# A shared expert's up product done with seven half-size products, its down products set between the next group's

## The chip, the cores and the metric

The kernel runs on one core of one Trainium2 chip. The metric is the device time of one execution in microseconds (us), lower is better. A profiled execution also leaves a trace; the times of all instructions in this document are from such executions, and windows are given in us from the start of the span.

The engines are TensorE (PE, with its weight loads shown apart as PEld), VectorE (DVE), ScalarE (ACT), GpSimd (POOL) and SyncE (SP, which here only issues transfers).

## The reference, cut to what matters

All tensors are float32. The input is x of 4 x 512 tokens of 512 values, so T = 2048 tokens and D = 512.

```python
# 1. a feed-forward layer whose expert (one of 4) goes by the token's id
h = layernorm(x)
x = x + where(expert_of(token_id) == e, (silu(h @ Wg[e].T) * (h @ Wu[e].T)) @ Wd[e], ...)   # Wg = Wu = Wd = ctx
# 2. a mixture of 32 experts, four a token, and a shared expert that all tokens pass
h = rmsnorm(layernorm(x), norm_w)
weights, ids = top_k(softmax(h @ gate_w), 4)
routed = sum over the four of weight * (silu(h @ w13[e][:, :256]) * (h @ w13[e][:, 256:])) @ w2[e]
shared = silu(h @ shared_gate_w) * (h @ shared_up_w) @ shared_down_w    # 512 -> 256 -> 512
out = x + routed + shared + layernorm(x)
```

The residual inside the second layer is its own normalised input, so the output is the sum of x, that input, the routed and the shared part. An expert takes at most a fixed number of tokens; the data here stay below it.

## The kernel before, in words

The 2048 tokens are 16 tiles of 128, and four tiles make a group (GT = 4, G = 4 groups of 512 tokens). There are three stages on the time axis.

**Cross attention layer, 0 to 173 us.** `xattn` (L499) loops over 19 blocks b of 128 tokens that share an expert. For each block TensorE makes `up(b)` (L453, `pp`, 32 instructions of 128 columns), then `down(b)` (L476, `po`, 512 columns), with transposes (`turn_block`, `tp`) between. VectorE makes the tokens' moments (`x_moments`, L336 to L339), copies the transposed tokens (`xT<-tp`, L450), the product `aT<-s,pp` (L474) and the sum into `acc` (L494). From block 5 on the second layer's start is woven in: `settle`, `norm` (L595, L607: the norms, whose powers POOL makes at L605), `turn_row` (L619, transposes to `h2T`, one tile per group, kept for all four groups), and for each finished group the routing: `route` (L648, 16 gate matmuls into `pc`, a ScalarE copy to `lT`), `choose` (L663, the transpose `pl` and the top four), `spread`, `count` (`pn`) and `number`, which give each token its slot in the experts' table.

**Shared expert, 173 to 269 us.** For each group, `glu_up` (L832) makes for the two halves f of the 256 inner values the gate product `pg` and the up product `pu`: four matmuls of 512 columns each over the four chunks c of D, so 16 a group, 4 x 128 x 512 multiplications each. ScalarE makes silu of `pg` (L847), VectorE the product with `pu` (L848, tile `aT_s`). Then `shared` (L860) makes the four tiles' down products (`glu_down`, L851, two matmuls of 512 columns a tile), which VectorE adds into `acc` (L864). The last group's transposes, routing and `ranks` (L775, the order of the experts by load, a long chain of small VectorE instructions) are called between group 0's up and down products. TensorE's order, like that of each engine, is made by a scheduler from the calls' order, so transposes, logits and downs of group 0 stand mixed.

Rows go to the experts' table (`s_dram`) by indirect transfers that POOL issues: `scatter_one(j, k)` (L754) sends tile j's rows to their k-th expert's slots, and `base(j)` (L764) sends a finished tile of `acc` to the output. In this stage they wait in a list `to_put`; `step(product)` (L770) takes the next from the list and has it wait for that product. `glu_up` calls it after every second matmul and `glu_down` after every tile, so 12 times a group.

**Ranks, 269 to 634 us.** The loop over 32 experts in order of load (L1214) takes each expert's rows (`fetch`, on SP's queue), transposes them on VectorE (L971), makes the up products (`up_rank`, L1041, 256 columns at most) and the down products (`down_rank_by_halves`, L1071), which already replace eight half products by seven with sums on VectorE. The results go out by POOL. Its weights come on SP's queue into the pools `wts_a` and `wts_b`, several ranks ahead. `wts_b` and `last` open when the pools of the shared stage close.

Two notes on tiles: `shw13` holds the shared gate and up weights side by side (128 x 4 x 512) and `shw2` the down weights; `ps_m` are three banks of PSUM (2 KB a partition), `ps_o` two and `ps_t` two.

Of the kernel before, what the change touches and what calls it, by code (L numbers as in the profile page):

```python
# [8 lines left out]
F32 = mybir.dt.float32  # L9
# [8 lines left out]
P = 128  # L18
# [41 lines left out]
def tile_xattn_moe(  # L60
# [38 lines left out]
    tok_sb = const.tile([P, NT], I32, name="tok_sb")  # L99
    nc.sync.dma_start(tok_sb, tok)  # L100
    acc = keep.tile([P, NT, D], F32, name="acc")
    cT = ctx_pool.tile([P, EX, DC, D], F32, name="cT")

    def context(e):
# [5 lines left out]
    nwq = const.tile([P, DC], F32, name="nwq")  # L110
    shw13 = keep.tile([P, DC, 2 * I], F32, name="shw13")
    shw2 = keep.tile([P, IC, D], F32, name="shw2")

    none = ctx_pool.tile([P, NB, RW], F32, name="none")

    def second_inputs(after_):

# [123 lines left out]
    nc.vector.tensor_reduce(xrow, xv.rearrange("p e t -> p t e"), AX.X, ALU.add)  # L241
    xblk, xq = split(xrow, ctx_pool, "x", F16)

    xa = ctx_pool.tile([P, NT, P], F16, name="xa")
    xbt = ctx_pool.tile([P, NT, NT], F16, name="xbt")
    xb16 = ctx_pool.tile([P, NT, NT], F16, name="xb16")
    nc.vector.tensor_tensor(
# [251 lines left out]
    def xattn():  # L499
        def fetched(*js):  # L500
            for j in js:
                x_block(j)

        fetched(0, 1, 2)
        for b in range(2):
            loaded = x_registers(b)
            with tc.issue_after(loaded) if loaded is not None else nullcontext():
                st = x_moments(b)
            behind(st, scaled if b else planned)
            if not b:  # L510
# [24 lines left out]
        for b in range(XB):  # L535
            j = GT * (b // 2 + 1)
            if j < NT and b % 2 == 0:
                for i in range(j, j + GT):
                    st = x_moments(i)
                    if i == GT:  # L540
                        behind(st, made[0])
                x_root(j, GT)
                if j == GT:
                    fetched(*range(2 * GT, NT))
                    second_inputs(st)
                    blanks(loads[-1])
            if b + 3 < XB:
                x_norm(b + 3)
                if not b:
                    behind(powers[-1], made[0])  # L550
            if 0 < b < XB - 2:
                hold(b + 2)
            if b + 1 < XB:
                up(b + 1, range(DC // 2))

            g, i = divmod(b - (XB - NT) - GT - 2, GT)
            if i == 0 and g >= 0:
                choose(g, ups_[-1])
# [12 lines left out]
            if j >= 1:  # L571
                norm(j - 1)
            if j >= 0:
                settle(j)
            if j >= GT + 4:
                scatter(j - GT - 4)
            for late_, what in ((3, spread), (4, number)):
                if j >= late_ and (j - late_) % GT == GT - 1:
                    if what is number:
                        count((j - late_) // GT)  # L580
                    what((j - late_) // GT)


    hs, h2T, tops = {}, {}, {}
    row_puts, out_puts, out_puts_l = [], [], []
    tails = []
# [61 lines left out]
    def route(g):  # L648

        pc = ps_t.tile([P, P], F32, tag="tp", name="pc")  # L650
        for c in range(DC):
            for i in range(GT):
                nc.tensor.matmul(
                    pc[i * E : (i + 1) * E, :],
                    gate_sb[:, c, :],
                    h2T[g][:, c, i * P : (i + 1) * P],
                    start=(c == 0),
                    stop=(c == DC - 1),
                )
        lT = tops[g] = mid.tile([P, P], F32, tag="lT", name=f"lT{g}")  # L660
        nc.scalar.copy(lT, pc)
# [102 lines left out]
    def base(j):  # L764
        return put_rows(out, xtok[:, j : j + 1], acc[:, j, :], out_puts, "base")
# [63 lines left out]
    HD = D // 2  # L829
    muls_s, adds_s = [], []  # L830

    def glu_up(xT, w13t, name):  # L832
        aT = cols.tile([P, IC, GT * P], F32, tag="aT", name=f"aT_{name}")
        for f in range(IC):
            pg = ps_m.tile([P, GT * P], F32, tag="mm", name="pg")
            pu = ps_m.tile([P, GT * P], F32, tag="mm", name="pu")
            for ps, fo in ((pg, f), (pu, IC + f)):
                for c in range(DC):
                    ins = nc.tensor.matmul(
                        ps, w13t[:, c, fo * P : (fo + 1) * P], xT[:, c, :], start=(c == 0), stop=(c == DC - 1)  # L840
                    )
                    if c % 2:
                        step(ins)
            if f == 0:
                first_half = ins
            s = mid.tile([P, GT * P], F32, tag="silu", name="s")
            nc.scalar.activation(s, pg, AF.Silu)  # L847
            muls_s.append(nc.vector.tensor_tensor(aT[:, f, :], s, pu, ALU.mult))  # L848
        return aT, first_half

    def glu_down(aT, w2t, i):  # L851
        po = ps_o.tile([P, D], F32, tag="po", name="po")
        for f in range(IC):
            ins = nc.tensor.matmul(  # L854
                po, aT[:, f, i * P : (i + 1) * P], w2t[:, f, :], start=(f == 0), stop=(f == IC - 1)
            )
        step(ins)
        return po

    def shared(g, aT):  # L860
        for i in range(GT):
            j = g * GT + i
            po = glu_down(aT, shw2, i)
            adds_s.append(nc.vector.tensor_tensor(acc[:, j, :], acc[:, j, :], po, ALU.add))  # L864
            to_put.append(lambda j=j: base(j))


    def blanks(after_):

        n = NS // (P * NB)  # L870
        ins = nc.sync.dma_start(
            s_dram[:NS, :].rearrange("(n p j) w -> p n (j w)", j=NB, p=P),
            none.rearrange("p j w -> p (j w)").unsqueeze(1).to_broadcast([P, n, NB * RW]),
        )
        behind(ins, after_, mybir.DependencyClass.Sync)

    xattn()
    aT_s = {}
    to_put.extend(lambda j=j, k=k: scatter_one(j, k) for j in range(NT - GT - 4, NT - GT) for k in range(K))
    aT_s[0], up_s = glu_up(h2T[0], shw13, "s0")  # L880
    rank_x = rank_rows(adds_x[-1])
    norm(NT - 1)
    turn_row(NT - 2, downs[-1])
    turn_row(NT - 1, up_s)
    route(G - 1)
    choose(G - 1)
    spread(G - 1)
    count(G - 1)
    number(G - 1)
    to_put.extend(lambda j=j, k=k: scatter_one(j, k) for j in range(NT - GT, NT) for k in range(K))  # L890
    first.close()
    late = ctx.enter_context(tc.tile_pool(name="late", bufs=2))
    wts_a = ctx.enter_context(tc.tile_pool(name="wts_a", bufs=2))
    third = ctx.enter_context(ExitStack())
    slots = third.enter_context(tc.tile_pool(name="slots", bufs=1))
    er, er_x, er_i, over_i = ranks()
    for g in range(G):
        if g:
            aT_s[g], _ = glu_up(h2T[g], shw13, f"s{g}")
        shared(g, aT_s[g])  # L900
    while to_put:
        to_put.pop(0)()

# [347 lines left out]
    with tc.If(need > 0):  # L1251
# [17 lines left out]
            return oh  # L1269

        def gathered(table, index, width, tag, name):
            pool = late if tag == "xg_x" else last
# [131 lines left out]
```

## Time and profile before

| what | us |
|---|---|
| median of three runs | 646.26 |
| lowest, highest | 644.96, 646.71 |
| the profiled execution | 647.86 |
| its span | 646.0 |
| TensorE busy in the span | 608.7 |
| VectorE busy | 397.3 |
| POOL busy | 246.2 |
| ScalarE busy | 216.0 |
| first shared product (L839) starts | 172.74 |
| last shared down product ends, rank 0's first matmul (L1050) starts | 268.76 |

The span runs from the first to the last instruction of the trace; 1.86 us of the execution lie around it. In a line of a timeline the first number is the start in us, the second the time from the first to the last of so many instructions (x8) that follow each other, then engine, line of the kernel, operation, what it writes and reads, and its size; in brackets stands how long the engine sat idle before it and what ended that wait. In a line of a table of windows, the busy time of the five rows PE, PEld, DVE, ACT and POOL follows the window, each with its number of instructions, then TensorE's granted clock as a share of full speed, the DMA engines' mean busy share and the GB/s moved.

### The profile page before, as it was taken

The numbers are of one execution on the slowest core, as the hardware profiler recorded it, in microseconds if no ns is written. First come the engines' busy times: TensorE is split into PE (matmuls) and PEld (weight loads), VectorE is DVE, ScalarE is ACT, GpSimd is POOL, SyncE is SP. The second block draws the span as 40 slices with busy tenths as digits, with TensorE's granted clock in tenths as the row PEclk, the third lists the DMA queues.
The fourth block names the chain that finished last, engine by engine and source line by source line (L and its number), as shares of the span: only waits on it lengthen the run. The fifth ranks groups of instructions, "written<-read, shape, count | busy, mean of one in ns | idle before, by whom it ended". The sixth has DMA issues, their size and how long they took to land. (4 is left out here: it accounts for less than half of the span.)

```text
span 646.0 us, 10595 instructions
## 1 busy us (share of the span) xinstructions
PE 608.7 (94%) x2962; PEld 433.5 (67%) x2962; DVE 397.3 (61%) x1113; ACT 216.0 (33%) x390; POOL 246.2 (38%) x217
## 2 busy tenths in 40 slices
PE   5899999999997999999999999999999999999990
PEld 2777767776543444566767687677678888888870
DVE  7655457575725712756667567667668777778730
ACT  2444765764322000122323222322333333333320
POOL 4451101365673555433234324324324232323331
PEclk9999999999997999999999999999999999999996
DMA  7489991335272697698979979979999999999442
GB/s 260 135 309 413 413 415 70 133 118 216 99 269 104 195 375 210 197 319 165 288 154 260 258 151 241 275 160 244 275 265 278 281 261 274 239 247 229 62 55 37
DMA packets 104453, 144.57 MB, mean 224 GB/s; under 512 B 21184, under 2 KB 58048, under 8 KB 101824
## 3 DMA queue, kind: packets, MB, share of 16 engines
q1 hardware_dynamic: 86400, 101.54, 53.6%
q0 software_dynamic: 17984, 42.26, 27.0%
q8 instruction: 26, 0.43, 0.3%
q14 instruction: 43, 0.35, 0.2%
HBM read 79.05 MB, written 66.22 MB: 225 GB/s over the span
## 5 line engine op out<-in xcount | busy, mean ns | idle before, releaser
L1022 POOL DMA_INDIRECT out<-eo,to_all x64 | 100.5, 1570 | 228.9 <-DVE eo L1091 111.3
L1050 PE MATMUL pg<-xT,w 128*128 128x256 f32 (+2 forms) x512 | 135.2, 377 | 0.0
L1050 PE MATMUL pu<-xT,w 128*128 128x256 f32 (+2 forms) x512 | 114.9, 376 | 0.0
L1088 ACT ACTIVATE eo<-po,wt 128x256 f32<-128x256 f32 x124 | 58.6, 474 | 158.5 <-PE po L1085 120.0
L1050 PEld LDWEIGHTS pg<-xT,w 128*128 128x128 f32 x512 | 96.5, 190 | 17.7 <-issue 5.4
L1050 PEld LDWEIGHTS pu<-xT,w 128*128 128x128 f32 x512 | 97.2, 190 | 12.2 <-issue 0.8
L636 POOL DMA_INDIRECT s_dram<-h,slot x64 | 62.2, 973 | 35.4 <-issue 15.4
L458 PEld LDWEIGHTS pp<-xT,held 128*128 128x128 f32 x576 | 66.8, 192 | 8.3 <-issue 5.2
L458 PE MATMUL pp<-xT,held 128*128 128x128 f32 x576 | 68.2, 276 | 1.4 <-DVE xT L450 0.8
L479 PE MATMUL po<-cT,aT 128*128 (+1 forms) x152 | 68.6, 593 | 0.3 <-issue 0.3
L971 DVE STREAM_TRANSPOSE xT<-z 128x1024 f32<-128x1024 f32 x32 | 65.3, 2041 | 3.8 <-DMA z<-s_dram 3.8
L1091 DVE SCALAR_TENSOR_TENSOR eo<-po,wt,eo 128x256 f32<-128x256 f32 x93 | 44.7, 482 | 16.2 <-PE po L1085 9.8
L1057 DVE TENSOR_TENSOR aT_r<-s,pu 128x256 f32<-128x256 f32 (+2 forms) x64 | 26.4, 414 | 41.0 <-PE pu L1050 35.4
L981 ACT ACTIVATE xT<-xT,nwq 128x256 f32<-128x256 f32 x64 | 29.1, 502 | 59.7 <-DVE xT L971 43.1
L479 PEld LDWEIGHTS po<-cT,aT 128*128 128x128 f32 x152 | 27.3, 190 | 27.9 <-issue 27.9
L1068 DVE TENSOR_TENSOR t_r<-w,t_r 128x256 f32<-128x256 f32 x62 | 26.3, 424 | 31.6 <-PE po L1085 29.0
L1085 PE MATMUL po<-t_r,aT_r 128*128 128x256 f32 x124 | 38.1, 389 | 2.0 <-DVE eo L1091 1.5
L605 POOL TENSOR_TENSOR rs<-rs,mhalf 128x2 f32<-128x2 f32 x16 | 11.3, 706 | 74.8 <-DVE rs L604 74.8
L1085 PE MATMUL po<-w,aT_r 128*128 128x256 f32 x124 | 39.7, 401 | 0.0
L389 ACT COPY held<-cT 128x1024 f32 x36 | 36.0, 1048 | 10.3 <-DVE valid L306 10.0
L1085 PE MATMUL po<-t_r,s_r 128*128 128x256 f32 x124 | 37.8, 387 | 0.4 <-DVE eo L1091 0.2
L854 PE MATMUL po<-shw,aT_s 128*128 128x512 f32 x64 | 32.3, 644 | 1.4 <-issue 1.0
(203 smaller groups left out, 765.2 us busy)
## 6 DMA issues: line engine op xcount, KB each, us to landing
w<-in_w SPq DMA_DIRECT2D x192, 256.0 KB
s_dram<-none SPq DMA_DIRECT2D x1, 20840.0 KB
z<-s_dram SPq DMA_DIRECT2D x128, 128.0 KB
h_dram<-h SPq DMA_DIRECT2D x4, 1042.0 KB
cT<-in_ctxT SPq DMA_DIRECT2D x4, 1024.0 KB
out<-none SPq DMA_DIRECT2D x1, 1024.0 KB
s_dram<-h,slot POOLq DMA_INDIRECT x64
out<-eo,to_all POOLq DMA_INDIRECT x64
```

The source lines that it names most:

```text
L389: ins = nc.scalar.copy(held[b][:, h : h + n], cT[:, bass.ds(e, 1), h : h + n].rearrange("p o c f -> p (o c) f"))
L458: ins = nc.tensor.matmul(ups[b][:, f, :], held[b][:, c, f * P : (f + 1) * P], xT_[b][:, c, :], start=(f == 0 and c == 0) if b == 0 else (c ...
L479: ins = nc.tensor.matmul(po, aT_[b][:, f, :], cT[:, bass.ds(off[b], 1), f, :].rearrange("p o f -> p (o f)"), start=(f == 0), stop=(f == DC ...
L636: put = nc.gpsimd.indirect_dma_start(out=table, out_offset=bass.IndirectOffsetOnAxis(ap=index, axis=0), in_=src, in_offset=None,)
L854: ins = nc.tensor.matmul(po, aT[:, f, i * P : (i + 1) * P], w2t[:, f, :], start=(f == 0), stop=(f == IC - 1))
L971: ins = nc.vector.transpose(xT.rearrange("p c (r b) -> p r c b", b=SQ), z.rearrange("p r (a c) -> p r c a", c=DC))
L981: nc.scalar.mul(xT[:, c, :], xT[:, c, :], nwq[:, c : c + 1])
L1022: put = nc.gpsimd.indirect_dma_start(out=out, out_offset=bass.IndirectOffsetOnAxis(ap=dst, axis=0), in_=eo, in_offset=None, bounds_check=T ...
L1050: last_up = nc.tensor.matmul(ps, w13t[:, c, f * P : (f + 1) * P], xT[:, c, :n], start=(c == 0), stop=(c == DC - 1))
L1085: return nc.tensor.matmul(ps, L[i], R[i], start=first_, stop=True, skip_group_check=True)
L1088: nc.scalar.mul(eo[i][:, j, :], ps, wt[:, i : i + 1])
L1091: nc.vector.scalar_tensor_tensor(eo[i][:, j, :], ps, wt[:, i : i + 1], eo[i][:, j, :], ALU.mult, ALU.add)
```

## The change

The up product of a group is seen as one matrix product: the weights, 512 values by 512 columns (256 gate, 256 up), against 512 values by 512 tokens. Both are cut in two by two blocks: the weights by halves of D and by gate and up, the tokens by halves of D and by halves of the group. Seven products of blocks (each 256 values x 256 columns x 256 tokens) with sums before and after them replace the eight that the plain product has. A product is four matmuls of 256 columns, so a group has 28 of them in place of 16 of 512 columns.

What moves with it:

- `shared_weights` makes four sums of weight blocks on VectorE, once, called at block 6 of the cross attention (one of them in place over a block of `shw13`).
- `shared_tokens(g)` makes for each group four sums of token blocks on VectorE, one of them at product 2 and two in place over blocks of `h2T`.
- `glu_up(g)` is now a generator of six steps. It uses three banks: ScalarE copies banks to `c11`, `c22`, `c12`, VectorE adds the next bank to the copy, and bank `u1` is accumulated over products 1, 6, 7 and 4.
- `shared(g, i)` makes one tile's down product, in the order 2, 3, 0, 1; each stands after one step of the next group's generator.
- `step` is called after each half product (14 a group) and after each down product (4), so 18 times a group.
- The pools `late`, `wts_a` and `slots` open, and the first stage's pool closes, ahead of the shared stage; a new pool `sums` holds the sums and copies. `none` and `xa` are only allocated earlier, and one buffer for a part that does not run here moves to `slots`.

```diff
@@ xattn, loop over b @@
+            if b == 6:
+                weight_sums.update(shared_weights())
@@
-    def glu_up(xT, w13t, name):
...
-    def glu_down(aT, w2t, i):
...
+    def shared_weights():
+        (a11, a12), (a21, a22) = [
+            [shw13[:, 2 * k : 2 * k + 2, i * I : (i + 1) * I] for k in range(2)] for i in range(2)
+        ]
+        s1, s2, s4 = [cols.tile([P, 2, I], F32, name=f"su{i}", bufs=1) for i in (1, 2, 4)]
+        plus(s1, a21, a22)
+        less(s2, s1, a11)
+        less(s4, a12, s2)
+        less(a21, a11, a21)
+        return {1: a11, 2: a12, 3: s4, 4: a22, 5: s1, 6: s2, 7: a21}
+
+    def shared_tokens(g):
+        (b11, b12), (b21, b22) = [
+            [h2T[g][:, 2 * k : 2 * k + 2, j * HALF : (j + 1) * HALF] for j in range(2)] for k in range(2)
+        ]
+        t1, t2 = [sums.tile([P, 2, HALF], F32, tag=f"st{i}", name=f"st{i}_{g}") for i in (1, 2)]
+        less(t1, b12, b11)
+        less(t2, b22, t1)
+        less(b12, b22, b12)
+        return {1: b11, 2: b21, 3: b22, 4: b21, 5: t1, 6: t2, 7: b12}
+
+    def product(ps, i, R, first_=False):
+        w = weight_sums[i]
+        for f in range(2):
+            for c in range(2):
+                ins = nc.tensor.matmul(
+                    ps[:, f, :],
+                    w[:, c, f * P : (f + 1) * P],
+                    R[i][:, c, :],
+                    start=first_ and f == 0 and c == 0,
+                    stop=f == 1 and c == 1,
+                    skip_group_check=True,
+                )
+            step(ins)
+        return ins
+
+    def glu_up(g):
+        R = tokens_s[g]
+        b1 = bank("u1")
+        product(b1, 1, R, True)
+        c11 = held_sum(b1, "c11")
+        yield
+        b2 = bank("u2")
+        product(b2, 2, R, True)
+        less(R[4], R[4], R[6])
+        plus(c11, c11, b2)
+        nc.scalar.activation(c11, c11, AF.Silu)
+        yield
+        b3 = bank("u3")
+        ins = product(b3, 5, R, True)
+        c22 = held_sum(b3, "c22")
+        yield ins
+        product(b1, 6, R)
+        c12 = held_sum(b1, "c12")
+        yield
+        product(b3, 3, R)
+        plus(c12, c12, b3)
+        nc.scalar.activation(c12, c12, AF.Silu)
+        product(b1, 7, R)
+        plus(c22, c22, b1)
+        aT = aT_s[g] = cols.tile([P, IC, GT * P], F32, tag="aT", name=f"aT_s{g}", bufs=1)
+        muls_s.append(nc.vector.tensor_tensor(aT[:, :, HALF:], c12, c22, ALU.mult))
+        yield
+        product(b1, 4, R)
+        if g + 1 < G:
+            tokens_s[g + 1] = shared_tokens(g + 1)
+        muls_s.append(nc.vector.tensor_tensor(aT[:, :, :HALF], c11, b1, ALU.mult))
+        yield
@@ after xattn() @@
+    first.close()
+    late = ctx.enter_context(tc.tile_pool(name="late", bufs=2))
+    wts_a = ctx.enter_context(tc.tile_pool(name="wts_a", bufs=2))
+    third = ctx.enter_context(ExitStack())
+    sums = third.enter_context(tc.tile_pool(name="sums", bufs=1))
+    slots = third.enter_context(tc.tile_pool(name="slots", bufs=1))
     to_put.extend(lambda j=j, k=k: scatter_one(j, k) for j in range(NT - GT - 4, NT - GT) for k in range(K))
-    aT_s[0], up_s = glu_up(h2T[0], shw13, "s0")
+    tokens_s[0] = shared_tokens(0)
+    ups_s = [glu_up(g) for g in range(G)]
+    next(ups_s[0])
+    next(ups_s[0])
+    up_s = next(ups_s[0])
+    next(ups_s[0])
     rank_x = rank_rows(adds_x[-1])
     norm(NT - 1)
     turn_row(NT - 2, downs[-1])
     turn_row(NT - 1, up_s)
+    next(ups_s[0])
     route(G - 1)
...
     er, er_x, er_i, over_i = ranks()
+    next(ups_s[0])
     for g in range(G):
-        if g:
-            aT_s[g], _ = glu_up(h2T[g], shw13, f"s{g}")
-        shared(g, aT_s[g])
+        for i in (2, 3, 0, 1):
+            if g + 1 < G:
+                next(ups_s[g + 1])
+            shared(g, i)
+        if g + 1 < G:
+            next(ups_s[g + 1])
+            next(ups_s[g + 1])
```

More of the change, by code (lines that the diff above doesn't have):

```diff
@@ L101, in tile_xattn_moe @@
     acc = keep.tile([P, NT, D], F32, name="acc")
+    none = ctx_pool.tile([P, NB, RW], F32, name="none")
+    xa = ctx_pool.tile([P, NT, P], F16, name="xa")
     cT = ctx_pool.tile([P, EX, DC, D], F32, name="cT")
@@ L112, in tile_xattn_moe @@
     shw2 = keep.tile([P, IC, D], F32, name="shw2")
-    none = ctx_pool.tile([P, NB, RW], F32, name="none")
     def second_inputs(after_):
@@ L242, in tile_xattn_moe @@
     xblk, xq = split(xrow, ctx_pool, "x", F16)
-    xa = ctx_pool.tile([P, NT, P], F16, name="xa")
     xbt = ctx_pool.tile([P, NT, NT], F16, name="xbt")
@@ L581, in xattn @@
                     what((j - late_) // GT)
+    weight_sums = {}
     hs, h2T, tops = {}, {}, {}
@@ L830, in tile_xattn_moe @@
     muls_s, adds_s = [], []
-    def glu_up(xT, w13t, name):
[L833 to L849, printed above, removed]
@@ L851, in glu_down, with plus, less @@
-    def glu_down(aT, w2t, i):
+    HALF = GT * P // 2
+    HD = D // 2
+    def plus(dst, x_, y_):
+        return nc.vector.tensor_tensor(dst, x_, y_, ALU.add)
+    def less(dst, x_, y_):
+        return nc.vector.tensor_tensor(dst, x_, y_, ALU.subtract)
+    def shared_weights():
[8 more added lines that the diff above has]
+        return {1: a11, 2: a12, 3: s4, 4: a22, 5: s1, 6: s2, 7: a21}
@@ new lines, in bank, with held_sum @@
+    def bank(name):
+        return ps_m.tile([P, 2, HALF], F32, tag="mm", name=name)
+    def held_sum(ps, name):
+        t = sums.tile([P, 2, HALF], F32, tag=name, name=name)
+        nc.scalar.copy(t, ps)
+        return t
+    def glu_up(g):
[30 more added lines that the diff above has]
+        yield
@@ L852, in glu_down, with shared @@
+    def shared(g, i):
+        j = g * GT + i
         po = ps_o.tile([P, D], F32, tag="po", name="po")
@@ L854, in glu_down @@
             ins = nc.tensor.matmul(
-                po, aT[:, f, i * P : (i + 1) * P], w2t[:, f, :], start=(f == 0), stop=(f == IC - 1)
+                po, aT_s[g][:, f, i * P : (i + 1) * P], shw2[:, f, :], start=(f == 0), stop=(f == IC - 1)
             )
         step(ins)
[L858 to L865, printed above, removed]
+        adds_s.append(nc.vector.tensor_tensor(acc[:, j, :], acc[:, j, :], po, ALU.add))
+        to_put.append(lambda: base(j))
     def blanks(after_):
@@ L877, in tile_xattn_moe @@
     xattn()
-    aT_s = {}
-    to_put.extend(lambda j=j, k=k: scatter_one(j, k) for j in range(NT - GT - 4, NT - GT) for k in range(K))
-    aT_s[0], up_s = glu_up(h2T[0], shw13, "s0")
+    first.close()
[4 more added lines that the diff above has]
+    slots = third.enter_context(tc.tile_pool(name="slots", bufs=1))
+    aT_s, tokens_s = {}, {}
+    to_put.extend(lambda j=j, k=k: scatter_one(j, k) for j in range(NT - GT - 4, NT - GT) for k in range(K))
+    tokens_s[0] = shared_tokens(0)
[4 more added lines that the diff above has]
+    next(ups_s[0])
     rank_x = rank_rows(adds_x[-1])
@@ L890, in tile_xattn_moe @@
     to_put.extend(lambda j=j, k=k: scatter_one(j, k) for j in range(NT - GT, NT) for k in range(K))
[L891 to L895, printed above, removed]
     er, er_x, er_i, over_i = ranks()
+    next(ups_s[0])
     for g in range(G):
-        if g:
-            aT_s[g], _ = glu_up(h2T[g], shw13, f"s{g}")
-        shared(g, aT_s[g])
+        for i in (2, 3, 0, 1):
[5 more added lines that the diff above has]
+            next(ups_s[g + 1])
     while to_put:
@@ L1271, in gathered @@
         def gathered(table, index, width, tag, name):
-            pool = late if tag == "xg_x" else last
+            pool = slots if tag == "xg_x" else last
             rows = pool.tile([P, 1, width], F32, tag=tag, name=name, bufs=2 if tag == "xg_x" else EO)
```

## The prediction, as written before the result was known

> **What bounds the kernel now.** I read the page's busy shares first, then a table of windows, then TensorE's timeline through the stage that the change touches, then the three engines around one hole in it.
>
> ```profile
> PE 608.7 (94%) x2962; PEld 433.5 (67%) x2962; DVE 397.3 (61%) x1113; ACT 216.0 (33%) x390; POOL 246.2 (38%) x217
> PEclk9999999999997999999999999999999999999996
> ```
>
> TensorE is busy for 94% of the span, and its granted clock has one dip, in the thirteenth slice of 16 us. The windows (PE, PEld, DVE, ACT, POOL, clock, DMA share, GB/s) place both:
>
> ```profile
> 180.00:200.00 20.00, 14.13 (x66) 6.53 (x66) 3.95 (x11) 4.48 (x9) 12.03 (x13) 0.92 0.60 227
> 200.00:220.00 20.00, 20.00 (x46) 8.76 (x45) 17.39 (x59) 2.69 (x4) 8.08 (x9) 0.91 0.32 123
> 220.00:240.00 20.00, 20.00 (x48) 8.72 (x47) 3.93 (x6) 1.20 (x2) 13.09 (x14) 1.00 1.02 363
> 240.00:260.00 20.00, 20.00 (x47) 8.66 (x46) 4.12 (x6) 1.20 (x2) 10.77 (x12) 1.00 0.71 216
> 300.00:320.00 20.00, 20.00 (x91) 13.47 (x90) 12.68 (x30) 5.23 (x11) 7.31 (x5) 1.00 1.02 233
> ```
>
> The shared stage (173 to 269) has TensorE full from 200 on; VectorE is full only from 200 to 220, with the routing and the ranks. The rank phase behind it has TensorE full too, although its DMA share stands near 1. TensorE's timeline gives the prices:
>
> ```profile
> 226.50 3.60 PE L839 MATMUL pg<-h2T,shw 128*128 128x512 f32 x8
> 229.93 3.60 PE L839 MATMUL pu<-h2T,shw 128*128 128x512 f32 x8
> 268.76 3.62 PE L1050 MATMUL pg<-xT,w 128*128 128x256 f32 x16
> 272.21 2.97 PE L1050 MATMUL pu<-xT,w 128*128 128x256 f32 x13
> ```
>
> A float32 matmul is two instructions here. Eight of 512 columns take 229.93 - 226.50 = 3.43 us, 0.858 per matmul; sixteen of 256 take 272.21 - 268.76 = 3.45, 0.431 per matmul. Half the columns cost half the time.
>
> ```profile
> 192.13 1.38 PE L854 MATMUL po<-shw,aT_s 128*128 128x512 f32 x2 [1.01 <-issue]
> 198.27 0.47 PE L667 MATMUL pl<-ident,lT 128*128 128x128 f32 x1 [4.75 <-ACT lT L661]
> 197.95 0.27 ACT L661 COPY lT<-pc 128x128 f32<-128x128 f32 x1 [8.35 <-remote]
> 196.00:198.00 2.00, 0.00 (x0) 0.00 (x0) 0.00 (x0) 0.05 (x1) 0.00 (x0) 0.71 0.34 133
> ```
>
> This is the hole. The copy of the last group's logits waits for a signal until 197.95, though the logits' matmuls are shown ending at 191.1; TensorE stands for 4.75 us, and no engine computes between 196 and 197.9. The other three groups' copies (93.7, 127.6, 161.3) came 1.2 us or less after their matmuls. I do not know the cause.
>
> **The change, part by part.** The sum is made on the profiled execution, 647.86 us (span 646.0 and 1.86 around it), which is 1.60 above the median of the runs, 646.26.
>
> 1. *Products.* A group had 16 matmuls of 512 columns, 16 x 0.858 = 13.73 us; it gets 7 x 4 of 256, 28 x 0.431 = 12.07. That is -1.66 for each of 4 groups, -6.6 in all, in a stage where TensorE is the bound. The 32 down matmuls stay.
>
> 2. *The hole.* From 191.12 (pc's end) to 193.51, TensorE did one matmul worth 0.86, so 1.5 lost; then 4.75; then the granted clock is 0.5 from 196.82 to 203.65, of which TensorE works 198.27 to 203.65, 5.4 us at half rate, 2.7 lost. Together 9.0. In the changed order the last group's logits follow product 7 and its two transposes, one matmul and then the transpose pl stand behind them, and the scatters beside them are in other places. Bounds: 0 (it comes again) and -9.0. I take -9.0 for the likeliest case, since three of four such copies ran without it, and give the other end a case of its own.
>
> 3. *Waits that go.* The down products waited 1.9 us in total for the last aT (weight loads of L854, 3 times) and TensorE itself 1.4; another group's products now stand between. -1.5.
>
> 4. *Waits that come*, by the changed order of each engine. (a) Tile 15's transposes wait for h, whose mean and root on VectorE and POOL now stand behind token sums of 0.69 us: 1.2 (0 to 2.5). (b) pl, own and the two pn meet less cover, since half products of 1.7 us stand where 3.4 us blocks stood: 2.0 (0.7 to 3). (c) Group 1's product 4 needs its bank read by the sum of c22, which on VectorE is queued behind what is left of the ranks chain: 1.7 (0.5 to 3.0, beyond that see the rivals). (d) The last group has no next group between its products 7 and 4 and its downs: 1.0 (0.3 to 1.5), from a sum of 0.69 and its hand-over. (e) Bank hand-overs: bank u1 is written by products 1, 6, 7 and 4 in turn, each after a reader of 0.6 to 0.69 us; in every group some five new hand-overs, mostly behind a down or another product. Nothing in the trace before has this form; the nearest row is the 0.28 us that a down product waited for an acc sum at 266.94. 20 x 0.1 = 2.0 (0 to 6). Sum +7.9 (1.5 to 16).
>
> 5. *Weight sums.* Four VectorE operations of 0.69 us, put by the scheduler into blocks 2 and 3 of the cross attention:
>
> ```profile
> 36.91 0.68 DVE L474 TENSOR_TENSOR aT<-s,pp 128x512 f32<-128x512 f32 x1
> 39.17 0.69 DVE L494 TENSOR_TENSOR acc<-acc,po 128x512 f32 x1 [1.59 <-PE po L479]
> 44.02 0.68 DVE L450 COPY xT<-tp 128x512 f32<-128x512 f32 x1
> 46.09 3.73 PE L458 MATMUL pp<-xT,held 128*128 128x128 f32 x32
> ```
>
> Three come after the mult at 36.91, where VectorE idles 1.59; three take 2.0, so the sum at 39.17 slips by some 0.5 and the copy xT, with the fourth, by up to 1.2. It ends at 44.7 and is needed at 46.09, so 1.4 of slack covers it. But they also wait for the gate's and the up weight's loads, whose transfers the queue's bytes put at about 36.4, an estimate; if these are late, x_moments, the xT copy and TensorE are late by as much. +0.8 (0 to 2.5).
>
> 6. *At nothing.* Token sums, bank sums and copies: VectorE 6 x 0.69 = 4.1 us a group more, ScalarE 3 copies and the same silu work, 1.8 more, beside 19 us of TensorE a group; VectorE has over 15 of 20 free from 220 on. Between 200 and 220 it has 2.6, which is why (c) is there. Scatters: 18 steps a group for 12, each 0.96 us on POOL's queue at 1.27 apart, so POOL alone now paces them; the last of s_dram moves from 240.7 to about 227, and the first fetch of z, at 243.5 on SP's queue, with it. The first transpose of z is at 262, so earlier gains nothing, and a delay of some 10 us would still be covered. Behind the scatters on POOL stand only tile 15's roots (in (a)) and the base rows. Pools that open earlier: SP's rank weights come some 9 us sooner; hidden.
>
> 7. *The way to the end.* The rank phase takes a shift whole if TensorE bounds it: it is busy 19.4 to 20 of 20 there, and waits 2.1 us in total for weights. So -6.6 - 9.0 - 1.5 + 7.9 + 0.8 = -8.4: 639.5 in a profiled execution, 637.9 against the median.
>
> [...] The row is 4.75 us of standing and then 6.83 us at 0.5. [...]
>
> **Rivals.** *The hole comes again* (0.30): its place, logits then one matmul then pl, keeps its form. While all stand, VectorE works off its queue, so (c) and part of (b), 2.0, are hidden: -8.4 + 9.0 - 2.0 = -1.4, 644.9, with +-2.
>
> *VectorE holds TensorE in the routing* (0.15, slower). In the trace, the routing and ranks run without a gap from 208.29 to 219.8, 11.5 us. If (c) waits for the whole chain, TensorE stands 11.5 in place of 1.7, and after a stand like the 4.75 above the clock halves, 5.4 us at half rate, 2.7: +12.5, 650.4. It decides from 5.7 + 1.7 = 7.4 us of standing on. For it: 17.39 of 20 busy. Against: between the ranks' pn and product 4 stand four products and three downs, 7 x 1.72 = 12 us of cover.
>
> *DMA sets the rank phase* (0.08): its share is 0.97 to 1.02 in several windows. Ranks that start earlier then wait for weights; half the gain stays, 642.0. Against: weights are issued four to five ranks ahead, paced by TensorE itself.
>
> **How the numbers follow.** The likeliest, 0.47, is 637.9; its own range, from the bounds of 4 and 5 without all falling one way, 634 to 642. Cases: 0.47, all faster by over 0.3% (1.94 us, about what a measurement here can tell from none); 0.30 around 644.9, of which 0.13 faster, 0.12 same, 0.05 slower; 0.08 at 642, 0.07 faster; 0.15 slower. Faster 0.67, same 0.13, slower 0.20. Below 634 lie 0.06, above 648.5 some 0.13, so the range is 634 to 648.5.
>
> **What would show it.** Right: L871 with 224 instructions of about 0.215 us; rank 0's first matmul near 260 instead of 268.76; no TensorE wait over 3 us and no half clock in 185 to 215; the same 365 us from there to the end. Wrong: a wait of ScalarE's copy lT for over 3 us (the hole); product 4 of group 1 waiting for VectorE over 3 us; L458 in block 3 starting after 46.9; weights waited for more than 2.1 us in the ranks.

## The result, and the profile after

The changed kernel takes 663.32 us (median of four runs, 660.92 to 665.68) against 646.49 (644.96 to 647.17) for the kernel before: a ratio of 1.0264, with a 95% interval of 1.0221 to 1.0306. It is slower by 16.8 us, where 8.4 us of gain were forecast. The kernel before itself takes about 637 us in some comparisons, called prompt below, and 644 to 648 in others, called late, and this first comparison is a late one, so every number stands beside that of the kernel before from the same comparison.

The changed kernel's profiled execution took 660.92 us, its span 659.1. Its page opens with

```profile
PE 607.7 (92%) x3058; PEld 455.0 (69%) x3058; DVE 415.1 (63%) x1145; ACT 223.0 (34%) x402; POOL 251.3 (38%) x217
PEclk9999999999987979999999999999999999999997
```

TensorE has about as much busy time as before (607.7 for 608.7), although its products need 6.6 us less, since more of its work runs at half clock. The table of windows (PE, PEld, DVE, ACT, POOL, clock, DMA share, GB/s) shows where:

```profile
180.00:200.00 20.00, 11.76 (x76) 9.04 (x75) 8.87 (x39) 6.37 (x12) 15.53 (x16) 0.80 0.65 250
200.00:220.00 20.00, 15.23 (x46) 10.14 (x46) 13.43 (x36) 3.65 (x6) 5.32 (x6) 0.86 0.22 85
220.00:240.00 20.00, 15.07 (x59) 10.84 (x58) 8.36 (x22) 1.45 (x3) 14.80 (x15) 1.00 0.97 333
240.00:260.00 20.00, 16.12 (x51) 10.62 (x52) 8.48 (x13) 2.81 (x5) 9.09 (x9) 0.83 0.70 236
```

Before, TensorE was busy for 20.00 of 20 from 200 to 260. Now it lacks four to eight in each window, and the clock falls in three, to a granted 0.50 (in the windows 193 to 201, 209.3 to 212.6 and 240 to 246): (1 - 0.80) x 20 x 2 = 8.0 us at half rate, then 5.6, then 6.8, 20.4 in all for 6.8 before. TensorE's timeline has the stands:

```profile
186.78 0.70 PE L871 MATMUL u<-h2T,shw 128*128 128x256 f32 x2
195.06 0.48 PE L669 MATMUL pl<-ident,lT 128*128 128x128 f32 x1 [7.58 <-issue]
195.33 1.92 PE L871 MATMUL u<-h2T,shw 128*128 128x256 f32 x4
197.93 4.60 PE L871 MATMUL u<-h2T,shw 128*128 128x256 f32 x10
209.45 0.19 PE L719 MATMUL pn<-own,tri 128*128 128x32 f16 x1 [4.77 <-DVE own L711]
233.18 1.89 PE L871 MATMUL u<-st,su 128*128 128x256 f32 x8
242.24 3.78 PE L928 MATMUL po<-shw,aT_s 128*128 128x512 f32 x4 [7.17 <-issue]
249.81 1.98 PE L928 MATMUL po<-shw,aT_s 128*128 128x512 f32 x4 [1.64 <-DVE acc L932]
284.62 3.62 PE L1130 MATMUL pg<-xT,w 128*128 128x256 f32 x16
```

The stage from the first shared product to rank 0's first matmul takes 284.62 - 173.27 = 111.4 us, for 96.0 before. The ranks behind it take 361.4 for 360.4 and the tail behind TensorE's last matmul 13.0 for 16.9. The stage also starts 0.5 us later. Together 0.5 + 15.3 + 1.0 - 3.9 = 12.9, which is the 13.1 us between the two spans but for rounding: the loss lies in the stage.

What do the other engines wait for in these stands? Their lines in the timeline:

```profile
194.74 0.27 ACT L663 COPY lT<-pc 128x128 f32<-128x128 f32 x1 [8.81 <-remote]
205.40 0.69 DVE L921 TENSOR_TENSOR aT_s<-c,u 128x512 f32<-128x512 f32 x1 [5.42 <-PE u L871]
241.50 0.69 DVE L932 TENSOR_TENSOR acc<-acc,po 128x512 f32<-128x512 f32 x1 [8.57 <-remote]
```

Each waits for a matmul that TensorE's record shows done long before. The logits' matmuls are shown ending at 186.8, and the copy starts at 194.74. Product 4's last matmul is shown starting at 197.93, and the product that reads it starts at 205.40. The down product whose sum starts at 241.50 is shown ending at 229.9; in the kernel before, 11 of the 16 such sums start 0.04 us after their matmul's shown end. TensorE's signals come late by 6 to 12 us: the updates of its semaphore that end the three waits are recorded at 194.72, 205.37 and 241.47, with four more behind the second by 205.59. TensorE stands because it needs what these readers make: pl needs lT; the count's pn needs own, which stands behind the product at 205.40 in VectorE's queue; the down product at 242.24 needs the bank that the sum at 241.50 frees. Whether the signal alone is late or the matmul's true end too, the trace cannot say.

Beside the first and the third stand, and up to 2 us before the second, POOL issues indirect transfers without a pause, 1.27 us apart (its own timeline, of the changed kernel):

```profile
235.03 0.96 POOL L638 DMA_INDIRECT s_dram<-h,slot  x1 [0.30 <-issue]
236.30 0.96 POOL L638 DMA_INDIRECT s_dram<-h,slot  x1 [0.30 <-issue]
237.56 0.96 POOL L638 DMA_INDIRECT s_dram<-h,slot  x1 [0.30 <-issue]
238.83 0.96 POOL L638 DMA_INDIRECT s_dram<-h,slot  x1 [0.30 <-issue]
```

Such a run lasts from 185.3 to 201.8 and from 220.7 to 243.9 here. In the kernel before it lasted from 179.5 to 194.7, ahead of its one hole and into it, and later only from 218 to 227. The end of its first run, with the next scatter 5 us behind it:

```profile
193.46 0.96 POOL L636 DMA_INDIRECT s_dram<-h,slot  x1 [0.30 <-issue]
194.73 0.96 POOL L636 DMA_INDIRECT s_dram<-h,slot  x1 [0.31 <-issue]
200.73 0.96 POOL L636 DMA_INDIRECT s_dram<-h,slot  x1 [5.04 <-PE po L854]
```

That gave theory S: while POOL issues indirect transfers back to back, TensorE's signals come late. Its rivals: W, the half-size products, bank hand-overs and mixed order make the stands; C, the hole belongs to the logits' matmuls. Later came V (signals are late in some comparisons only), and O, D and M on the ranks.

### The profile page after: what moved, and what is told of

Same layout as the page of the kernel before. It is cut to its first block, busy times and chain, and to the rows that moved or that the text cites. A ratio compares the mean times of both kernels' runs of the same rounds, so it can differ in the third digit from the quotient of the medians.

```text
span 659.1 us, 10831 instructions
## 1 busy us (share of the span) xinstructions
PE 607.7 (92%) x3058; PEld 455.0 (69%) x3058; DVE 415.1 (63%) x1145; ACT 223.0 (34%) x402; POOL 251.3 (38%) x217
## 4 chain that ended last, share of the span: by engine, by line
PE 65%; DMA 9%; issue 8%; DVE 7%; POOL 6%; SPq 3%; ACT 0%; DVEq 0%; POOLq 0%
PE pu L1130 12%; PE pg L1130 12%; PE po L1165 12%; PE u L871 8%; PE pp L457 5%; PE po L478 5%; DMA w<-in_w 4%; PE po L928 4%; POOL s_dram L638 3%; PE pp_x L1210 3%; SPq L1004 2%; DMA z<-s_dram 2%; DVE xT L1051 2%; PE po L1234 1%; DMA acc<-in_x,xtok 1%
## 5 line engine op out<-in xcount | busy, mean ns | idle before, releaser
L1102 POOL DMA_INDIRECT out<-eo,to_all x64 | 101.9, 1593 | 223.9 <-DVE eo L1171 105.0
L638 POOL DMA_INDIRECT s_dram<-h,slot x64 | 63.9, 999 | 32.2 <-issue 16.3
L457 PEld LDWEIGHTS pp<-xT,held 128*128 128x128 f32 x576 | 66.8, 192 | 8.2 <-issue 5.2
L457 PE MATMUL pp<-xT,held 128*128 128x128 f32 x576 | 68.2, 276 | 1.4 <-DVE xT L449 0.8
L1171 DVE SCALAR_TENSOR_TENSOR eo<-po,wt,eo 128x256 f32<-128x256 f32 x93 | 44.7, 481 | 16.4 <-PE po L1165 9.8
```

Of the source, the lines that this page charges most:

```text
L457: ins = nc.tensor.matmul(ups[b][:, f, :], held[b][:, c, f * P : (f + 1) * P], xT_[b][:, c, :], start=(f == 0 and c == 0) if b == 0 else (c ...
L638: put = nc.gpsimd.indirect_dma_start(out=table, out_offset=bass.IndirectOffsetOnAxis(ap=index, axis=0), in_=src, in_offset=None,)
L1102: put = nc.gpsimd.indirect_dma_start(out=out, out_offset=bass.IndirectOffsetOnAxis(ap=dst, axis=0), in_=eo, in_offset=None, bounds_check=T ...
L1171: nc.vector.scalar_tensor_tensor(eo[i][:, j, :], ps, wt[:, i : i + 1], eo[i][:, j, :], ALU.mult, ALU.add)
```

## The experiments

### Releases at other rates: four kernels where the kernel before took 637

A release is one call of `step`, which sets one scatter free. The first kernel has one release for each of the seven products of a group in place of two (the expectations call such a product a half product).

```diff
     def product(ps, i, R, first_=False):
...
-            step(ins)
+        step(ins)
         return ins
```

> The changed kernel, but a half product releases a scatter once, at its end, and not after each of its two halves: 11 releases a group, 1.72 us apart, in place of 18. Theory S (while POOL issues indirect transfers back to back, TensorE's signals arrive late, and who waits for them stands): in group 0 POOL still works off a backlog back to back, so the stand after the logits stays, while the stand of 7.2 us at 235 and its half clock go: 650 us, 646 to 655. Theory W (half products, bank hand-overs and the mixed order make the stands, whatever POOL does): as the changed kernel, 663, 659 to 667.

The second also leaves out every second one of the first 11 releases, and the third does the same (of the first 12) in the kernel before.

```diff
+    passed = []
+
     def step(product):
+        passed.append(product)
+        if len(passed) <= 11 and len(passed) % 2:
+            return
         if to_put:
```

> As the run with one release a half product, and in the first 11 releases only every second one, so that POOL has no backlog in group 0 either. Theory S: no stand of TensorE over 3 us and no half clock in the shared stage, 639 us, 635 to 645. Theory W: 663, 659 to 667.

> The kernel before the change, with every second release of the first 12 left out, so that POOL issues at most every 3.4 us in group 0. Theory S: the stand of 4.75 us after the logits and the half clock behind it go: 646.5 - 9 = 637.5, 635 to 641. Theory C (the stand belongs to the logits' matmuls, the copy and the transpose behind them, not to POOL): 646.5, 644 to 648.

The fourth is the kernel before with a release after every up matmul.

```diff
                 for c in range(DC):
                     ins = nc.tensor.matmul(
...
-                    if c % 2:
-                        step(ins)
+                    step(ins)
```

> The kernel before the change, with a release after every up matmul and every tile's down product, 20 a group in place of 12, so that POOL issues back to back in groups 1 and 2 too. Theory S: late signals and a stand there as in the changed kernel, 654 us, 650 to 662. Theories W and C: 646.5, 644 to 648.5.

Measured: 638.03 (ratio 1.0011, 0.9974 to 1.0048), 656.10 (1.0263, 1.0214 to 1.0313), 652.01 (1.0210, 1.0166 to 1.0255) and 637.31 (0.9989, 0.9956 to 1.0022), with the kernel before at 637.34. Nothing is as any theory had it. The kernel before was 9 us shorter than at first, about the price of its hole, and no trace of the four has the hole, a late signal or a half clock up to the last shared down product, though POOL issues back to back in the fourth from 179 to 242 but for gaps of up to 3.5 us. So dense transfers alone do not make signals late. Theory V came from this: something that differs between comparisons must be added.

The two runs with fewer releases lost in the ranks: from rank 0's first matmul to TensorE's end they take 382.7 and 377.7 us, for 361.0 in the fourth and 366.2 in the first. The waits of TensorE show a second bound, of the first run and of the second:

```profile
PE pg L1130 <- DVE xT L1057: 3.2, 1, 3.2
PE tp_x L1223 <- DVE a_x L1217: 1.0, 1, 1.0
```

```profile
PE pg L1135 <- issue: 3.8, 1, 3.8
PE pg L1135 <- ACT xT L1066: 2.4, 1, 2.4
```

The ranks wait for their turned rows. The first run's shared stage is 82.7 us long for 86.9 in the fourth, so 4.2 us were gained there and 5.2 given back.

### The changed kernel again, and without waits on products

> The changed kernel once more, beside the kernel before on the same chip. Theory V (TensorE's late signals belong to some chips or sessions, in which both kernels have them, the changed one two or three times and the kernel before once): where the kernel before takes about 637, without its hole, the changed one has none either, its shared stage takes 83 us for 87, and it takes 632, 629 to 636; where the kernel before takes about 646, the changed one takes 663. Theory W (the changed order makes the stands itself): 1.026 times the kernel before on any chip.

> The kernel before, for its trace on this chip. Theory V: no hole at 191 to 198 if it takes about 637, the shared stage then 87 us long for 96; the hole is there if it takes about 646. A fixed cause in the program (theory C): the hole is there in either.

```diff
     def step(product):
-        if to_put:
+        if False:
             behind(to_put.pop(0)(), product, mybir.DependencyClass.Sync)
```

> The changed kernel with no scatter released in the shared stage: all 48 are issued behind it, so the ranks start late and the time is some 60 us longer; only the shared stage is read. Theory S (indirect transfers issued back to back make the signals late): on any chip no late signal and a stage of 82 us or less from the first shared product to the last down product. Theory W: stands as in the changed kernel, 111 us.

Here the kernel before took 648.47. The changed one took 664.56 (1.0260, 1.0191 to 1.0329), the kernel before once more 647.43 (0.9993, 0.9953 to 1.0032) with its hole back: the copy lT at 199.02 after 8.77 of waiting. TensorE's own stand before pl is only 2.20 there, but it also stops for 0.44 and 1.09 us between the last matmuls of the logits themselves, with no wait shown. 664.56 is V's and W's number alike.

The third, 665.14, did not do what its expectation says. Without a wait on a product the scatters were free to be issued early, and POOL sent them back to back from 185 to 205 and 220 to 243. It has four stands, of 6.2, 6.8, 4.2 and 5.0 us. So the stands do not need a scatter's wait on a product.

### The scatters held, and dense ones in the kernel before, where it took 647

The first kernel adds to the edit just shown:

```diff
     while to_put:
-        to_put.pop(0)()
+        behind(to_put.pop(0)(), adds_s[-1], mybir.DependencyClass.Sync)
```

> The changed kernel, all 48 scatters of the shared stage held until its last down product is added: POOL issues no indirect transfer between 179 and the end of the stage. The ranks start some 60 us late; only the shared stage is read, to its last down product. Theory S (the signals are late because POOL issues indirect transfers back to back): where the kernel before takes about 647 too, no stand of TensorE over 2 us, no half clock, and a stage of 80 to 86 us. Theory W (the new order and the bank hand-overs make the stands): 105 us or more, with three stands, where the kernel before takes 647.

> The changed kernel as it is. Where the kernel before takes about 637 beside it: theory V (both kernels are without late signals there) 632, 629 to 636; theory W 654. Where the kernel before takes about 647: 664 by both.

> The changed kernel with one release a half product, once more. Where the kernel before takes about 637: 638 as measured. Where it takes about 647: theory S, the run of indirect transfers back to back in groups 1 and 2 is broken up, so the stands there go and the one in group 0 stays: 652, 647 to 657; theory W: 664 as the changed kernel.

> The kernel before with 20 releases a group, POOL issuing back to back through the stage. Where the kernel before takes about 637: 637 as measured. Where it takes about 647: theory S, late signals through groups 1 to 3 and further stands: 656, 651 to 664; theory W, 647 as the kernel before.

The kernel before took 646.66. With the scatters held (724.33 us in all, as the ranks start late), the changed stage is clean. POOL issues its last early scatter at 185.6 and the next indirect transfer at 256.7. Its windows:

```profile
200.00:220.00 20.00, 20.00 (x77) 14.45 (x76) 16.04 (x39) 3.02 (x5) 0.00 (x0) 1.00 0.64 211
220.00:240.00 20.00, 20.00 (x77) 14.37 (x76) 7.77 (x12) 3.02 (x5) 0.00 (x0) 1.00 0.01 1
```

From the first shared product to the end of the last down product it takes 81.7 us, at full clock and with no wait of TensorE over 1 us. Beside it, unheld, the changed kernel took 657.68 (1.0148, 1.0037 to 1.0259), with its stands. The half-size products, the banks and the calls' order are the same in both: W falls.

One release a product took 649.78 (1.0061, 1.0017 to 1.0105): the later stands are gone, the one behind the logits (4.0 us) stays, as S had it. The kernel before with dense releases, 637.31 where signals were prompt, took 671.09 (1.0355, 1.0255 to 1.0455). Its waits of TensorE:

```profile
PE pl L667 <- ACT lT L661: 14.9, 1, 14.9
PE po L853 <- DVE aT_s L847: 10.0, 2, 6.6
```

No line of the up product differs there from the kernel before, only the times of the releases. The same kernel has no late signal in the prompt comparison. So both are needed: indirect transfers issued back to back, and a late comparison. What makes a comparison late, no run shows; the first two sets of experiments were made on a chip of the same number, the first prompt, the second late. Nor do the runs part POOL's issuing from the writes that it starts. Traffic as such is not enough: between 60 and 97 us of the kernel before the DMA moves 413 to 415 GB/s without an indirect transfer, and the first copy of logits, at 93.74, starts 0.07 us after its matmuls.

The traces themselves tell late from prompt, in more than the stage. In all 14 late traces 182 to 237 of the some 2,000 semaphore updates of TensorE, VectorE and ScalarE have no record of their own (207 of 2,020 in the first trace of the kernel before, 194 of 2,065 in that of the changed one); in the six prompt ones none is missing. None is missing either where POOL issues no indirect transfer: from 60 to 120 us in the kernel before (205 of 205) and from 200 to 240 with the scatters held (81 of 81), while the changed kernel's first trace has 73 of 90 there. So indirect transfers go with disturbed signals, or a disturbed record of them, also far behind the stage (in the kernel before, 17 of 78 updates between 500 and 520 us have no record), and two of the stands shown, those at 195.06 and 242.24, are put down to "issue" and end with a signal that has no record: the copy lT is shown ending at 195.00 and the sum at 242.19, and neither's update is recorded. The times of these comparisons all come with a span and a granted clock, as a profiled execution gives them. Whether recording takes part in the delay is therefore a rival that no run tests.

### Why the ranks gave the gain back

The first kernel has one release a product, and:

```diff
     def up_block(xT, ws, name, after_=None, turned_=None):
...
-        nc.vector.tensor_tensor(a, s, pp[:, I:], ALU.mult)
+        ins = nc.vector.tensor_tensor(a, s, pp[:, I:], ALU.mult)
+        if turned_ is not None:
+            behind(ins, turned_)
```

> The changed kernel with one release a half product, and in the rank loop the block's product a_x set behind the next rank's transpose on VectorE, where the scheduler had set it before (a step order, no wait). Theory O (with later scatters the scheduler sets that transpose behind a_x, and TensorE then stands 4 us in rank 3 or 4, with a half clock behind it): the rank phase 361 to 363 us from rank 0's first matmul to TensorE's end in place of 366 to 371; 633.5 where the kernel before takes 637, 643 where it takes 647. Rival D (the transfers of the ranks' rows and weights set that stand, so it only moves): 638 and 649.

The next also leaves out the first four releases, and the third makes both edits in the kernel before.

```diff
     def step(product):
+        passed.append(product)
+        if len(passed) <= 4:
+            return
```

> As the pinned one, with the first four releases left out, so that POOL works off less of a backlog in group 0. Theory S: where the kernel before takes 647, the stand behind the logits and its half clock go too: 637, 634 to 641; where it takes 637, as the pinned one, 633.5. Theory C (the stand behind the logits has its own cause): 643 where the kernel before takes 647.

> The kernel before with its first four releases left out and a_x pinned in the same way; the up product as it was. Theory S: where the kernel before takes 647, its hole shrinks or goes: 638 to 643; where it takes 637: 637, 635 to 640. Theory C: 647 and 637.

> The changed kernel as it is, beside the others. Where the kernel before takes about 637, theory V: 632, 629 to 636; theory W: 654. Where it takes about 647: 656 to 664.

The kernel before took 646.71; the four took 649.00 (1.0025, 0.9987 to 1.0062), 657.25 (1.0162, 1.0117 to 1.0206), 652.78 (1.0079, 1.0044 to 1.0115) and 659.48 (1.0209, 1.0137 to 1.0282). Theory O falls: with a_x pinned the stand in the ranks moved, as rival D had it. The pinned kernel's line in TensorE's timeline:

```profile
359.45 6.21 PE L1210 MATMUL pp_x<-w,xT_x 128*32 128x512 f32 x32 [8.85 <-DMA w<-in_w]
```

Its ranks take 371.5 us, and its stand behind the logits 6.8 us. That stand varies between executions: four late traces of the unaltered changed kernel have 7.6, 9.1, 6.8 and 4.0 us. Without the first four releases it is 2.5 us in the changed kernel (its scatters then bunch from 234 to 251, and a stand of 5.0 follows there), and the kernel before has none over 1 in the stage: its copy follows the logits by 0.04 us, where two other late traces of it have 6.83 and 4.98. So C falls too. But the last scatter to the table, from which on the ranks' rows can be fetched, comes at 247.3 and 239.7, and the ranks take 379.1 and 374.7.

Most traces then fit one rule, model M: TensorE's end is the later of rank 0's first matmul + 361 and the last scatter to the table + 388 to 395 (398 in one run). Two lie outside it: without waits on products TensorE ends 365.0 us after rank 0's start, 4 later than the rule has it, and with the scatters held some 14 later. The rule is a fit; which transfer holds the ranks in each case was not followed.

| kernel (us of the kernel before beside it) | last table scatter | rank 0 | TensorE's end | from scatter | from rank 0 |
|---|---|---|---|---|---|
| before, first profile | 240.7 | 268.8 | 629.2 | 388.5 | 360.4 |
| changed, first profile | 240.1 | 284.6 | 646.0 | 405.9 | 361.4 |
| one release a product (637) | 232.6 | 255.0 | 621.2 | 388.6 | 366.2 |
| before, dense releases (637) | 227.9 | 259.0 | 620.0 | 392.1 | 361.0 |
| one release a product (647) | 239.4 | 261.7 | 632.3 | 392.9 | 370.6 |
| pinned (647) | 241.2 | 263.5 | 635.1 | 393.9 | 371.5 |
| without the first four (647) | 247.3 | 266.6 | 645.6 | 398.3 | 379.1 |

By this rule the kernel before lies on both bounds at once. A shorter shared stage then gains only if the last table scatter comes earlier too, and issuing the scatters earlier means issuing them densely, which in late comparisons went with late signals of TensorE (a stand of 14.9 us in the kernel before with dense releases).

### A paced kernel, and the changed one with prompt signals

The releases are left out in the first three products, the others have one each, and five products of the next two groups get a second one; a_x is pinned as above.

```diff
-            step(ins)
+            n = len(made_s)
+            if n >= 3 and (f or n in (7, 9, 11, 15, 18)):
+                step(ins)
+        made_s.append(ins)
```

> The changed kernel with a_x pinned, its releases paced: none in the first three half products, then one a half product and one a down product, and a second one in five half products of the two next groups, so that the last scatter to the experts' table is issued no later than with one a half product. Model M (TensorE's end is the later of two: rank 0's first matmul + 361, and the last scatter to the table + 388 to 395): with rank 0 at 256 and that scatter at 235, TensorE ends at 625 and the whole takes 640 where the kernel before takes 647, 635 to 645; 634, 631 to 638, where it takes 637. Theory S for group 0: the stand behind the logits is under 3 us. Against both: 649 and 638 as with one release a half product.

> The changed kernel as it is, beside the paced one. Where the kernel before takes about 647: 656 to 664, with late signals again. Where it takes about 637: model M, with rank 0 at 255 and the last scatter to the table at 227, TensorE's end at 616 and 631 in all.

> The paced kernel once more. Where the kernel before takes about 637: 632 as measured. Where it takes about 647: model M with theory S, no stand over 3 us in the shared stage, 640, 635 to 645; if dense transfers are not what makes the signals late, stands as in the changed kernel and 655 or more.

The kernel before took 636.74 in the first of these comparisons. The changed kernel took 631.19, a ratio of 0.9932 (0.9893 to 0.9971), 0.7% less, as model M had it: its last table scatter is at 226.8, rank 0 at 254.4, TensorE's end at 616.0. Its windows show POOL as busy with scatters as in the first profile or more, and TensorE full:

```profile
180.00:200.00 20.00, 19.23 (x111) 13.85 (x109) 18.58 (x62) 8.86 (x16) 15.64 (x15) 1.00 0.64 241
200.00:220.00 20.00, 20.00 (x78) 14.54 (x77) 15.00 (x36) 3.04 (x6) 15.52 (x15) 1.00 0.93 324
220.00:240.00 20.00, 20.00 (x75) 13.98 (x74) 7.41 (x11) 3.58 (x6) 15.13 (x16) 1.00 0.92 324
```

The paced kernel took 632.17 there (0.9936, 0.9903 to 0.9969), no less than the unpaced one, and 640.13 where the kernel before took 644.57 (0.9935, 0.9902 to 0.9968). The unpaced one was not run beside that last; in the other late comparisons it took 1.5 to 2.6% more than the kernel before. The 640 of the expectation holds; its "no stand over 3 us" does not, as one of 3.9 is left:

```profile
190.01 0.48 PE L669 MATMUL pl<-ident,lT 128*128 128x128 f32 x1 [3.94 <-ACT lT L663]
```

The trace shows seven scatters in a row from 179.6 to 187.8 ahead of it, the first four of them called in the cross attention, which the pacing does not touch. So the change with paced releases and a_x pinned gains some 0.65% in both kinds of comparison, 4.6 us in the prompt and 4.4 in the late one. Its two traces end 385.2 and 385.1 us after the last table scatter and 360.2 and 360.1 after rank 0's start: the second bound of model M is 385 or less, so the kernel before, at 388.5, had some 3 us of room on it.

## Why the prediction was wrong, point by point

- *Products, -6.6: right.* In the changed profile 24 instructions from 222.84 to 228.02 take 5.18 us, 0.216 each as priced. Where signals are prompt the stage takes 82.3 us (254.39 - 172.07), 4.6 less than the 86.9 of the kernel before with dense releases.
- *The hole, 0 or -9.0: the step that failed.* I bounded it by its own absence and its own return, and left no room for more holes, though I did not know its cause. It came again (7.58 us) and brought two more stands of 4.77 and 7.17. The clue was in the trace shown: the copy's wait was "remote" while the logits' matmuls were shown done 6.8 us before that wait ended, and POOL had issued back to back until 195.7. I held "three of four copies ran without it" for odds, but the other three stood behind runs of four scatters or none.
- *Scatters, costed at nothing: failed with it.* I wrote that POOL alone now paces the releases, and priced POOL's time. What it cost was TensorE's: the stage grew by 15.3 us here, and one stand of the kernel before with dense releases is 14.9 us long.
- *The first fetch of z, "a delay of some 10 us would still be covered": right for the first transpose, wrong for the ranks behind it.* Where the first fetch moved from 233.6 to 246.1 (the kernel before with dense releases, and with the early ones left out), the first transpose came at 254.6 and 254.2, yet TensorE ended 16.4 us later. The last table scatter sets a second bound on the end; with it at 245.4, the second run took 19 us more than the kernel before beside it.
- *Ranks, the shift passes whole:* right while the scatter bound is not reached (361.4 for 360.4), wrong beyond it. The "365 us from there to the end" reaches to 633.7, where the granted clock falls; TensorE's last matmul ends at 629.2, and the span at 646.0.
- *New waits, +7.9, and waits that go, -1.5: too large.* Where signals are prompt, TensorE waits 1.5 for own, 0.8 for the sum before product 4 and 0.5 for a bank in the whole stage. The bank hand-overs (2.0) hardly show.
- *Weight sums, +0.8: no cost to be seen.* In the first comparison the shared stage starts 0.5 us later (173.27 for 172.74) and L457's block at 46.60 for 46.09, but TensorE lost most of that ahead of it, in a wait of 0.73 at 43.60 for one of 0.31, and the same kernel's block starts anywhere from 45.52 to 46.88 in late traces. Where signals are prompt, it starts at 45.42, for 45.44 in the kernel before with dense releases.
- *At nothing: a miscount.* The change adds seven VectorE operations a group, not six (four token sums, three bank sums; 28 of the 32 more in the profile, the other four being weight sums).
- *Rivals.* "The hole comes again", at 644.9, had the mechanism by half and the price for one hole. "VectorE holds TensorE in the routing" would have been read into the wait for own, 4.77, but VectorE itself waited for TensorE's signal, 5.42. "DMA sets the rank phase" came true where the scatters are late: 8.85 us of waiting for weights in the pinned kernel.
- *Where no signal is late*, the gain is 5.5 us (631.19 against 636.74). The forecast of -8.4 would have had the right sign there by luck of the sum: the hole's 9.0 are not there to be had, and the products' 6.6 less some 2 of waits would make the 4.6 of the stage. The kernel before itself has no prompt trace, so how the 5.5 divide is not shown.

The changed kernel's half-clock stretches in the stage are 10.24, 3.41 and 6.83 us long, and each begins 4.5 to 4.9 us into a stand of 4.8 to 7.6 us. In the first trace of the kernel before, the clock falls 3.3 us into the stand of 4.75. Not every fall has a long stand before it: in the second trace of the kernel before, the clock falls at 194.66, when TensorE's longest gap in the stage so far was 1.09 us. By the windows 20.4 us lie at half rate.

## What to carry to other kernels

Give a hole whose cause is unknown a price for coming twice, and look at what every engine does during it, also the one that is only issuing transfers. Where a waiter starts microseconds after its matmul's shown end, as the copy lT did here (8.0 us), look for indirect transfers back to back beside it, spread them out, and measure the kernel before in the same comparison. And before shortening a stage, work out what else must be finished by its end: here, by model M, the last scatter bounded the end nearly as tightly as TensorE did (some 3 us of room).

## What the runs showed of the hardware that was not expected

- In late comparisons, and in no prompt one, TensorE's signals come late while GpSimd issues indirect transfers 1.27 us apart. The copy of the last logits starts 2.85 to 9.45 us after its matmuls' shown end beside runs of three to seventeen, and 16.67 us after it beside a run of twenty. Once it follows by 0.04, with a run of eight over for 1.7 us. Where the scatters stand some 1.7 us apart, with no more than four back to back (one release a product, from 195 us on), the signals are prompt: no wait of TensorE there is over 0.8 us. The same programs, with dense transfers, show no late signal in a prompt comparison: no wait of TensorE in the stage is over 0.8 us in the changed kernel and none over 0.3 in the kernel before with dense releases.
- In late comparisons 9 to 12% of the three engines' semaphore updates have no record in the trace, and none is missing in the two stretches without indirect transfers that were counted (205 of 205 and 81 of 81 recorded). Whether recording takes part in the delay is open.
- Between prompt and late comparisons the kernel before goes from 637 to 647 and the changed kernel from 631 to between 658 and 665, so which of the two is the faster depends on it.
- The stands do not need a scatter's wait for a matmul (4.2 to 6.8 us long without such waits, in one execution).
